# Taking the reciprocal roots of the 128-column norms on GpSimd instead of ScalarE and VectorE

## The chip, the cores and the metric

The kernel runs on one core of a Trainium2 chip. A core has TensorE (matrix multiply, PE in the profile), VectorE (DVE), ScalarE (ACT), GpSimd (POOL) and SyncE (SP, which here only starts transfers). Each engine works through its own instruction list in order, and they wait for each other through semaphores. The metric is the device time of one execution in microseconds.

## The reference

Two transformer layers over x of shape (8, 256, 128), that is 2048 rows of 128 columns, all in float32. Each layer has an attention block and a feed-forward block, and after each block the sum with its input is normalized:

```python
def _layernorm(x, axis=-1, eps=1e-05):
    m = jnp.mean(x, axis=axis, keepdims=True)
    v = jnp.var(x, axis=axis, keepdims=True)
    return (x - m) / jnp.sqrt(v + eps)

x = _layernorm(x + _L0_attn_ref(x, ...), axis=-1)   # Taylor-exp linear attention, 16 heads, RMS norm per head
x = _layernorm(x + _L0_ffn_ref(x, ...), axis=-1)    # top-1 of 2 experts plus a shared one, relu
x = _layernorm(x + _L1_attn_ref(x, ...), axis=-1)   # softmax attention, 16 heads of 8, rotary, causal
x = _layernorm(x + _L1_ffn_ref(x, ...), axis=-1)    # top-2 of 8 experts, silu gate
```

## The kernel before

The 2048 rows are worked in four groups (g = 0 to 3) of 512 rows; a group is a tile of 128 partitions by four row blocks of 128 columns. Layer 0's attention runs over eight batches with four steps each. As its groups become ready, layer 0's feed-forward network (`ffn0`, names ph, hq, pf), layer 1's attention (sa, sb, pr, pa, mx, qm) and layer 1's routed network (pg, sg, hT, pd, yg) follow, interleaved.

The routed network of a group works so: `gates`, `ranks` and `places` compute each row's two slots; GpSimd writes the rows to their slots in DRAM by indirect transfers (`sent`, L1025, slots<-x_b, for the last group slots<-pay); SP loads the slots in chunks (xg<-slots) and the weights of each slot tile's expert (we<-in_e, L1293); TensorE computes pg (L1329), ScalarE the silu (sg, L1335), VectorE the product hT (L1336), TensorE pd (L1353), and ScalarE copies yg out, which SP stores to DRAM (answers<-yg). For groups 0 to 2 GpSimd then gathers each row's two answers (L1417, yb<-answers); VectorE sums them, norms them, and SP stores the result (out<-yb). For the last group GpSimd scatters the answers (L1381), SP loads them, and two halves of the group are summed and normed.

A norm is made by `spreads` and `scaled_rows`. `spreads` takes mean and variance of each of the four row blocks on VectorE (L283, L284, into mv), the root of variance plus epsilon on ScalarE (L286, into sd) and its reciprocal on VectorE (L288, into rs). `scaled_rows` then subtracts and multiplies on VectorE, four instructions (L297). There are seventeen such norms: four of layer 0's attention (tiles named a), four of its network (f), four of layer 1's attention (b) and five of its network (o: groups 0, 1 and 2, and two halves of group 3, which have two row blocks each). The RMS norms inside layer 0's attention (L473, L481) are others, with 32 columns, and keep their root on ScalarE.

[...]The compiler puts an ACT_TABLE_LOAD ahead of an activation whose function isn't in the set at hand. In layer 1 ScalarE also computes Exp (L907, L1149), Tanh (L1339) and Silu (L1335), so that the root has loads on both sides there; a load is shown under the line of the activation that it stands before.

The order of the work: in layer 0's attention the lists of TensorE, ScalarE, VectorE and SP are in the order in which the program is written; in the second half TensorE's alone is, by the slot table of `second_half`, and a scheduler orders the other engines. GpSimd's list is the scheduler's throughout.

Of the kernel before, what the change touches and what calls it, by code (L numbers as in the profile page):

```python
# [11 lines left out]
F32 = mybir.dt.float32  # L12
BF16 = mybir.dt.bfloat16
I32 = mybir.dt.int32
AF = mybir.ActivationFunctionType
ALU = mybir.AluOpType
AX = mybir.AxisListType

P = 128
B, T, D = 8, 256, 128  # L20
NT = B * T // P
TG = 4
# [13 lines left out]
LN_EPS = 1e-5  # L36
# [43 lines left out]
def network(  # L80
# [19 lines left out]
    nc = tc.nc  # L100
# [3 lines left out]
    cpool = ctx.enter_context(tc.tile_pool(name="const", bufs=1))  # L104
# [3 lines left out]
    spool = ctx.enter_context(tc.tile_pool(name="stat", bufs=4))  # L108
# [122 lines left out]
    def column(name, value):  # L231
        t = cpool.tile([P, 1], F32, tag=name, name=name)
        nc.gpsimd.memset(t, value)
        return t

    eps_ln = column("eps_ln", LN_EPS)
    eps_rms = column("eps_rms", RMS_EPS)
    rt_half = column("rt_half", math.sqrt(0.5))


# [34 lines left out]
    def layernorm(r, name, y=None):  # L275
        return scaled_rows(r, name, spreads(r, name), y)

    def spreads(r, name):
        n = r.shape[1]
        mv = spool.tile([P, n, 2], F32, tag="mv", name=f"mv_{name}")  # L280
        for t in range(n):
            st = spool.tile([P, 6], F32, tag="bn", name=f"bn_{name}_{t}")
            nc.vector.bn_stats(st, r[:, t, :])  # L283
            nc.vector.bn_aggr(mv[:, t, :], st)  # L284
        sd = spool.tile([P, n], F32, tag="sd", name=f"sd_{name}")
        nc.scalar.activation(sd, mv[:, :, 1], AF.Sqrt, bias=eps_ln)  # L286
        rs = spool.tile([P, n], F32, tag="rs", name=f"rs_{name}")
        nc.vector.reciprocal(rs, sd)  # L288
        return mv, rs

    def scaled_rows(r, name, spread, y=None):
# [309 lines left out]
    def ffn0(g, buf, pbank, obank, even):  # L601
# [50 lines left out]
        def ended():  # L652
            pt = pbank(f"pb_{g}")
            for t in range(TG):
                w = slice(t * P, (t + 1) * P)
                nc.tensor.transpose(pt[:, w], got["y"][:, w], ident)
            r = got["r"] = gpool.tile([P, TG, D], F32, tag="r", name=f"r1_{g}")
            nc.vector.tensor_add(r, pt.rearrange("p (t d) -> p t d", t=TG), xs[g])
            got["s"] = spreads(r, f"f{g}")
# [47 lines left out]
    def second_half():  # L707
# [262 lines left out]
        def ended1(b):  # L970
            g, s = b // 2, b % 2
            yT = yTs.pop(b)
            po = bank(f"pz_{b}")
            for q in range(2):
                nc.tensor.matmul(
                    po[:, q * P : (q + 1) * P],
                    yT[:, q * P : (q + 1) * P],
                    wo1_sb,
                    start=True,
                    stop=True,  # L980
                )
            if s == 0:
                rs[g] = gpool.tile([P, TG, D], F32, tag="r", name=f"r2_{g}")
            nc.vector.tensor_add(
                rs[g][:, 2 * s : 2 * s + 2, :],
                po[:, : 2 * P].rearrange("p (q d) -> p q d", q=2),
                xs[g][:, 2 * s : 2 * s + 2, :],
            )
            if s == 1:
                at(6 * (b + 2) + 4, normed1, g, spreads(rs[g], f"b{g}"))  # L990
# [603 lines left out]
```

## Time and profile before

| | us |
|---|---|
| median of 3 runs | 611.17 (610.21 to 614.69) |
| the profiled execution | 610.17 |
| its span, first to last instruction | 608.4 |
| ScalarE: ACT_TABLE_LOAD | 21 of 1.283 each |
| ScalarE: root of a norm (sd) | 17 of 0.297 each |
| VectorE: reciprocal of a norm (rs) | 17 of about 0.18 each |
| GpSimd: indirect transfers L1025, L1417, L1381 | 71, 0.96 to 0.99 each |

The granted TensorE clock was 0.938 on average. In the profile a row of the timeline gives the start, the duration, the engine, the line, the operation with its tiles, how many were merged, and in brackets how long the engine was idle before and what ended that. The chain of waits is the work that ended last, followed backwards from the end; "issue" in it is time in which nothing that the profile shows was waited for. The slices cut the span in 40 equal parts of 15.2 us.

### The profile page before, as it was taken

The page shows a single profiled execution, that of the slowest core. Times are in us where ns is not written, and L with a number is a line of the kernel's source. Part 1 is how long each engine was busy: PE and PEld are TensorE (multiplying, and loading weights), DVE is VectorE, ACT ScalarE, POOL GpSimd, SP SyncE. Part 2 cuts the span into 40 slices and gives each one's busy share as a digit, 9 for nine tenths or more (in the row PEclk, how much of TensorE's full clock was granted, in tenths as well). Part 3 has the DMA queues.
Part 4 walks back from the last instruction along what each step waited for, and adds up shares of the span by engine and source line. Part 5 has one row for each costly group of instructions (what it writes and reads, how often), then busy time and mean ns, then how long its engine had stood idle before and what let it go on. Part 6 is the DMA issues. An engine that isn't in the chain of part 4 may idle for free.

```text
span 608.4 us, 10761 instructions
## 1 busy us (share of the span) xinstructions
PE 524.0 (86%) x4194; PEld 340.6 (56%) x4194; DVE 327.6 (54%) x759; ACT 248.1 (41%) x367; POOL 170.1 (28%) x208
## 2 busy tenths in 40 slices
PE   5799999999989999899989989899999859748750
PEld 2455656666654544344554546456678659748740
DVE  2346678478565162744564555746955436632424
ACT  2276444636341124144446344345547318322130
POOL 5022212222230030012213112452172540451670
PEclk9799999999999999989999996799999879998785
DMA  9106803230250000000000000231226357729512
GB/s 321 61 1 170 216 19 70 71 72 6 66 141 0 1 0 2 0 2 0 1 1 1 1 1 2 75 100 32 70 94 195 105 154 211 233 82 260 168 41 70
DMA packets 40562, 47.34 MB, mean 78 GB/s; under 512 B 3655, under 2 KB 29404, under 8 KB 39488
## 3 DMA queue, kind: packets, MB, share of 16 engines
q1 hardware_dynamic: 37520, 40.33, 23.8%
q0 software_dynamic: 2560, 5.02, 2.5%
q10 hardware_dynamic: 432, 1.31, 0.6%
q8 instruction: 34, 0.56, 0.4%
q14 instruction: 16, 0.13, 0.1%
HBM read 35.95 MB, written 11.15 MB: 77 GB/s over the span
## 4 chain that ended last, share of the span: by engine, by line
PE 65%; DVE 14%; POOL 6%; DMA 5%; ACT 5%; issue 4%; SPq 1%; POOLq 0%; ACTq 0%; DVEq 0%
PE pf L640 6%; PE pg L1329 6%; PE ph L622 5%; PE pv L356 5%; PE py L436 5%; PE sb L897 4%; PE pd L1353 4%; PE po L516 4%; DVE mx L860 4%; PE sa L828 3%; PE s L397 3%; PE pr L758 3%; POOL yb L1417 2%; PE pa L930 2%; PE py L444 2%
## 5 line engine op out<-in xcount | busy, mean ns | idle before, releaser
L1329 PE MATMUL pg<-xTs,we 128*128 128x128 f32 x480 | 66.8, 293 | 26.7 <-DVE hT L1336 14.5
L1329 PEld LDWEIGHTS pg<-xTs,we 128*128 128x128 f32 x480 | 61.7, 206 | 29.5 <-DVE hT L1336 15.5
L909 POOL TENSOR_SCALAR_AFFINE_SELECT pr<-pr 128x512 f32<-128x512 f32 (+1 forms) x48 | 37.7, 795 | 127.7 <-ACT pr L907 127.4
L460 POOL TENSOR_TENSOR y<-y 128x512 f32<-128x512 f32 x32 | 35.1, 1096 | 135.3 <-DVE y L453 103.4
L860 DVE TENSOR_REDUCE mx<-sa 128x4 f32<-128x1024 f32 (+1 forms) x48 | 56.5, 1219 | 27.3 <-PE sa L851 19.7
L414 DVE SCALAR_TENSOR_TENSOR at<-at,causal 128x1024 f32<-128x1024 f32 x32 | 39.2, 1225 | 42.2 <-ACT at L413 42.0
L413 ACT ACTIVATE at<-s,rt_half 128x1536 f32<-128x1536 f32 x32 | 49.2, 1536 | 17.7 <-PE s L405 17.7
L907 ACT ACTIVATE pr<-sb 128x1024 f32<-128x1024 f32 x48 | 46.5, 1021 | 17.3 <-PE sb L897 17.2
L897 PE MATMUL sb<-qm,kr 32*128 32x128 f32 (+1 forms) x512 | 34.6, 353 | 8.1 <-DVE mx L860 7.9
L436 PE MATMUL py<-at,v 128*64 128x256 f32 x256 | 41.1, 400 | 0.6 <-DVE at L414 0.3
L356 PE MATMUL pv<-wv,xt 128*128 128x512 f32 x64 | 35.3, 652 | 2.1 <-DVE kT L349 1.4
L640 PE MATMUL pf<-hq,w 128*128 128x512 f32 x72 | 37.0, 605 | 0.0
L516 PEld LDWEIGHTS po<-wo_sb,y 128*128 128x128 f32 x256 | 30.8, 192 | 9.6 <-issue 4.2
L1353 PE MATMUL pd<-e,hT 128*128 x240 | 35.1, 292 | 0.6 <-issue 0.3
L897 PEld LDWEIGHTS sb<-qm,kr 32*128 32x128 f32 x512 | 22.8, 189 | 20.1 <-DVE mx L860 17.2
L1417 POOL DMA_INDIRECT yb<-answers,slot_i x24 | 23.0, 960 | 39.4 <-DMA answers<-yg 27.2
L516 PE MATMUL po<-wo_sb,y 128*128 128x128 f32 x256 | 32.1, 278 | 1.9 <-DVE st L471 1.5
L1353 PEld LDWEIGHTS pd<-e,hT 128*128 128x128 f32 x240 | 31.5, 203 | 1.9 <-issue 1.1
L1025 POOL DMA_INDIRECT slots<-x_b,slot_i x24 | 23.3, 971 | 27.9 <-DVE nets L1244 22.2
L1335 ACT ACTIVATE sg<-pg 128x512 f32<-128x512 f32 (+1 forms) x24 | 13.5, 563 | 36.6 <-PE pg L1329 36.5
L930 PE MATMUL pa<-pr,vaug 128*32 128x128 f32 (+1 forms) x512 | 28.3, 338 | 0.0
L634 DVE TENSOR_SCALAR hq<-ph,sml 128x512 f32<-128x512 f32 x20 | 14.9, 749 | 22.7 <-PE ph L622 22.7
(228 smaller groups left out, 932.6 us busy)
## 6 DMA issues: line engine op xcount, KB each, us to landing
we<-in_e SPq DMA_DIRECT2D x60, 256.0 KB, 3.3
bc<-nr SPq DMA_DIRECT2D x14, 512.0 KB, 5.6
slots<-empty SPq DMA_DIRECT2D x3, 960.0 KB, 10.3
answers<-yg SPq DMA_DIRECT2D x21, 128.0 KB, 3.1
xg<-slots SPq DMA_DIRECT2D x9, 256.0 KB, 3.4
w<-in_w SPq DMA_DIRECT2D x2, 768.0 KB, 7.1
xt<-in_xt SPq DMA_DIRECT2D x4, 256.0 KB, 9.3
x<-in_x SPq DMA_DIRECT2D x4, 256.0 KB, 8.8
```

The source lines that it names most:

```text
L356: nc.tensor.matmul(pv, xT[:, t * P : (t + 1) * P], wv_sb[:, w], start=True, stop=True)
L413: nc.scalar.activation(at, ps[:, :, 0:SC], AF.Square, bias=rt_half, scale=SQ_SCALE)
L414: nc.vector.scalar_tensor_tensor(at[:, :, 0 : 2 * P], at[:, :, 0 : 2 * P], 0.5, causal.unsqueeze(1).broadcast_to([P, 4, 2 * P]), ALU.add, ...
L436: nc.tensor.matmul(py[o, cc], v[:, 0, w], at[:, i, :].rearrange("p (a q) -> p a q", q=P)[:, 0::2, :], start=True, stop=False,)
L516: nc.tensor.matmul(po, ys[b, c // 2][:, c % 2, q * P : (q + 1) * P], wo_sb[:, c, :], start=(c == 0), stop=(c == 7),)
L640: nc.tensor.matmul(got["o"], w2_sb[:, k * P : (k + 1) * P], hq.pop(n), start=(n == 0), stop=(n == 11),)
L860: nc.vector.tensor_reduce(mx[:, 2 * h : 2 * h + 2, 3 * js.start : 3 * js.stop - 2 : 3], ps[h].rearrange("p i (j k) -> p i j k", j=js.stop ...
L897: nc.tensor.matmul(ps[i // 2][:, i % 2, jj * wd : (jj + 1) * wd], kT[r, j, k], qms[b][r, j // 3, q], start=True, stop=True,)
L907: nc.scalar.activation(w, ps[h], AF.Exp)
L930: nc.tensor.matmul(pa[r, jj, :] if m == 0 else pa[r, jj, P:T], va[:, t + m, 4 * i + j, :], prs[b, jp][:, i, jj * T : (jj + 1) * T] if m == ...
L1329: nc.tensor.matmul(ph[:, b, cw], w[:, cw], x, start=True, stop=True)
L1353: nc.tensor.matmul(po[:, a * P : (a + 1) * P], hT[m][:, a, c * P : (c + 1) * P], e3_sb[:, bass.ds(net_i, 1), c * D : (c + 1) * D].rearrang ...
```

## The change

The column of LN_EPS is gone, and a tile of four columns of -0.5 is filled once. In `spreads` GpSimd adds the epsilon to the variance and raises the sum to the power of -0.5; the root on ScalarE, the reciprocal on VectorE and the tile sd are gone.

```diff
-    eps_ln = column("eps_ln", LN_EPS)
     eps_rms = column("eps_rms", RMS_EPS)
+    minus_half = cpool.tile([P, TG], F32, tag="minus_half", name="minus_half")
+    nc.gpsimd.memset(minus_half, -0.5)
     rt_half = column("rt_half", math.sqrt(0.5))
...
             nc.vector.bn_stats(st, r[:, t, :])
             nc.vector.bn_aggr(mv[:, t, :], st)
-        sd = spool.tile([P, n], F32, tag="sd", name=f"sd_{name}")
-        nc.scalar.activation(sd, mv[:, :, 1], AF.Sqrt, bias=eps_ln)
         rs = spool.tile([P, n], F32, tag="rs", name=f"rs_{name}")
-        nc.vector.reciprocal(rs, sd)
+        nc.gpsimd.tensor_scalar_add(rs, mv[:, :, 1], LN_EPS)
+        nc.gpsimd.tensor_tensor(rs, rs, minus_half[:, :n], ALU.pow)
         return mv, rs
```

In the built order of the changed kernel GpSimd has 34 instructions more, ScalarE 32 fewer (17 roots and 15 table loads) and VectorE 17 fewer. TensorE's order is unchanged. On SP the store out<-yb of group 1 and one answers<-yg store move ahead of the first xg load of group 3, and two weight loads with them. On GpSimd the two new instructions of a norm stand where the scheduler put them among the old ones; those of group 1's last norm stand behind the eight scatters slots<-pay.

## The prediction

> **What bounds the kernel now.** I read four views: the page's busy table with its slices, the chain that ended last, each engine's timeline around the seventeen norms, and the built order of both kernels.
>
> ```profile
> PE 524.0 (86%) x4194; PEld 340.6 (56%) x4194; DVE 327.6 (54%) x759; ACT 248.1 (41%) x367; POOL 170.1 (28%) x208
> PE   5799999999989999899989989899999859748750
> PEclk9799999999999999989999996799999879998785
> POOL 5022212222230030012213112452172540451670
> ```
>
> TensorE is full to about 480 us (slice 32), then has holes. Up to there a norm costs only what it delays on a chain of VectorE work that feeds TensorE. After it the chain is a queue on GpSimd:
>
> ```profile
> 521.73 1.28 ACT L1335 ACT_TABLE_LOAD   x1 [3.39 <-PE pg L1329]
> 528.21 1.28 ACT L286 ACT_TABLE_LOAD   x1
> 535.48 0.30 ACT L286 ACTIVATE sd_o<-mv_o,eps_ln 128x4 f32<-128x4 f32 x1 [5.99 <-DVE mv_o L284]
> 535.80 1.28 ACT L1335 ACT_TABLE_LOAD   x1
> ...
> 522.78 0.95 POOL L1417 DMA_INDIRECT yb<-answers,slot_i  x1 [27.21 <-DMA answers<-yg]
> ...
> 532.79 0.99 POOL L1025 DMA_INDIRECT slots<-pay,slot_i  x1 [0.30 <-issue]
> ...
> 541.69 0.96 POOL L1025 DMA_INDIRECT slots<-pay,slot_i  x1 [0.30 <-issue]
> 547.01 0.19 POOL L1312 COPY gs<-xg 128x4 f32<-128x4 f32 x1 [4.36 <-DMA xg<-slots]
> 547.14 0.18 POOL L1314 CAST di<-xg 128x4 int32<-128x4 f32 x1
> ```
>
> Two things: ScalarE sits from 528.2 to 535.5 at a root whose input is late, with its queue shut behind it; and GpSimd issues sixteen transfers in a row, 1.26 us apart, up to 542.65. The chain shows what one norm costs, first a plain one, then one behind a table load:
>
> ```profile
> 176.16 0.30 ACT sd_a L286
> 176.47 0.02 issue
> 176.49 0.19 DVE rs_a L288
> 176.68 0.03 issue
> 176.71 1.11 DVE x_a L297 x4
> ...
> 359.53 1.28 ACT L286
> 360.81 0.01 issue
> 360.83 0.30 ACT sd_b L286
> ```
>
> **The change part by part.** Removed: 17 roots on ScalarE of 0.30 us, 17 reciprocals on VectorE of 0.18, and, by the built order, 15 of the 21 table loads, 15 x 1.28 = 19.2 us of ScalarE. Added: 17 additions and 17 powers on GpSimd. The totals matter little, since neither engine is the bound; the latency from the statistics to the scaling of the rows does.
>
> Old latency: 176.14 (statistics end) to 176.71, 0.57 us. New latency: GpSimd wakes 0.07 us after VectorE (chain, 226.98 to 227.05 before rk), the addition takes 0.19 (the 128x4 COPY above), a hand-over of about 0.1 (taken from that wake-up) since the built order has the power wait on GpSimd's own semaphore, the power w, and 0.04 to wake VectorE: 0.40 + w.
>
> No row shows a power. From below it is the COPY of the same shape, 0.19. From above I use the row[...]: an indirect transfer makes its 128 descriptors in about 0.96 us, 7.5 ns each, so 512 powers taken one by one would be 3.8 us, 4.0 with the fixed part. The elementwise row L460 costs 1096 ns for 512 columns, 2.1 ns a column. If a power is a chain of some forty such steps (an assumption), four columns cost 0.34, so w = 0.19 + 0.34, about 0.5. I take 0.5, as the work is elementwise like L460, and keep 0.19 and 4.0. Then the new latency is 0.90, 0.33 more than the old.
>
> Norms, in time order, for w = 0.5:
> - Layer 0 attention, 96.4 and 137.2: the scaled rows aren't needed at once, but the causal multiply L414 stands behind them on VectorE and starts at 98.22 with no idle before it; TensorE's L436 follows it at once. The root is also taken off ScalarE, where L413 waited behind it, but VectorE's own order hides that. 0.2 each, 0.4. The third (176.1) is on the chain: 0.33.
> - First routed-network norm (215.3): in the new order its addition and power on GpSimd stand on either side of the second vaug memset (1.8 us), and its scaling on VectorE comes after x0T and one hq; the transpose that needs it runs at 221.16. The cover of some 4 us is nearly used up: 0.5. The attention norm at 220.5 is covered by 2.82 us of VectorE idle before 225.31; without that it would cost 0.33.
> - The next three of these (253.9, 305.4, 366.6) are on the chain: 3 x 0.33 = 1.0. The loads around 303 and 310 save no chain time that the trace shows.
> - Layer 1 norm at 358.9: GpSimd is in affine_select until 359.64, then 0.19 + 0.1 + 0.5 + 0.04 gives scaling at 360.47 instead of 361.37: 0.9 saved. At 415.3 likewise: affine_select until 415.80, scaling at 416.63 instead of 416.95: 0.3 saved. At 459.5 TensorE leads the chain on both sides: 0.
> - 503.6 to 512.8: four loads and two roots (5.7 us) leave ScalarE, which was busy 8.82 of 9.20 us; but TensorE was busy 9.02 of it, so what shows is its small gap at 512.5 to 512.8 and a little after: 0.5 saved. Both powers run before GpSimd's gathers resume at 522.78, with 10 us to spare.
> - 522.8 to 542.65: sixteen issues on GpSimd, untouched: 0.
> - Group 1's last norm (535.45): its addition is built behind the eight scatters, so VectorE, in order, stands until about 543.6 where it went on at 536.0. Behind it wait hT (537.72 before), so the next pg on TensorE, and on SP the out store. The order of SP changes too: that store, an answers store and two weight loads now come ahead of xg, which stood first. The weight load that ended TensorE's wait at 548.48 was issued at 544.97; it now goes at about 546.6 and lands after 3.47, at 550.1: 1.6 late. Against that, pg of the units before it now runs at 544.6 to 548.4, directly ahead, so TensorE is warm for what comes next, which took 2.08, 1.71 and 1.60 us in the cold stretch at 548.48 (granted clock 0.84 over 545 to 566) and about 0.9 each elsewhere: up to 2.7 back. I book 0, between -0.5 and +2.
> - Tail after 598.02: three norms one after another. VectorE now stands at each (in the new order the first scaling is ahead of the second half's statistics): 3 x 0.33, plus some 0.3 for statistics that no longer fill the gaps: 1.3.
>
> Sum: 0.4 + 0.33 + 0.5 + 1.0 - 0.9 - 0.3 - 0.5 + 0 + 1.3 = +1.8 us. The profiled execution took 610.17 (span 608.4), so 612.0; the median of 611.17 is 1.0 above it, so 613. Some twelve norms lie where w counts one for one (two, one, three, two, one and three above), so each us of w is worth 12 us: w = 0.19 gives 609, w = 0.86 makes +6, w = 2 gives 631, w = 4 gives 655.
>
> **Two rules of the Trainium skill.** The rows: the load at 415.11 begins 0.02 after the exp before it and the root starts at 416.40, 1.29 later, no drain in between. "ScalarE: Activation LUTs", What ACT_TABLE_LOAD costs, adds a drain of 1.38 us to every switch, 2.66 in all. By that, each of the two layer 1 norms would gain 1.38 more and the sum would be -1.0; by the trace it is +1.8. I use the trace. The rule that speaks against the change: the first y of L460 on GpSimd (28.22) took 1.04 us, like the later ones. "GPSIMD Engine Reference", Instruction dispatch, says that the first call of a freshly loaded routine pays about 6 us, unseen in a profile. If the power were such a routine, VectorE would stand some 6 us at the first norm, and the sum would be +7.8, 619. No loading row of GpSimd is in this trace, so I book nothing for it.
>
> **Rivals.** (1) The power is slow. Place: the VectorE queue at twelve norms. Price: 12 us for each us of w above 0.5. It decides from w = 0.86, where the loss passes 1%. Likely case w = 1.5, 625. For: no row shows a power cheap, and the page's GpSimd rows cost 1.6 times VectorE's for the same tile (L460 1096 ns, L507 686 ns where not held up). Against: only four columns. (2) ScalarE's freed time counts in full: 0.9 + 1.3 at the layer 1 norms, 5.7 at 503 to 513 and half of the 7.3 us stall at 528 to 535: about 9 less, 602. For: ScalarE is in the chain at 510.16 with a load. Against: TensorE was 98% busy there, and VectorE's new stall replaces ScalarE's old one. (3) The place behind the scatters is not made up for by a warm TensorE: 2 us there, and the later xg load and the answers stores behind it 4 more: 619. That the change doesn't do what it says is ruled out by the built order.
>
> **How the numbers follow.** About 1% (6.1 us) is what can be told from no change here. Chances: forecast 0.46, slow power 0.37, queue place 0.08, ScalarE in full 0.09. So faster 0.09, same 0.46, slower 0.45. The forecast's own range is 608 to 617; the range goes from 605, short of rival 2, to 630, w near 2, which leaves out about 2 in 10.
>
> **What would show it.** A row for the power on GpSimd with its mean (0.5, or over 0.86); VectorE idle before the scaling, ended by GpSimd, of 0.6 to 0.8 at plain norms; six table loads left; that idle of some 8 us once, near 535 to 543, with the out store ahead of xg on SP; pg after 550 at 0.9 instead of 2.08. I am wrong if a plain norm costs no more than 0.57, or if the stretch from 522 to 556 shrinks or grows by more than 2 us.

## The result, and the profile after

The changed kernel takes 627.99 us (median of six runs, 625.85 to 628.42) against 611.56 for the kernel before in the same session: a ratio of 1.0258, interval 1.0229 to 1.0288. The profiled execution took 625.85, its span is 623.9, 15.5 more than before. The sum of the prediction, +1.8 us, was made for a power of 0.5 us. The loss came as its first rival describes it, and is about twice what that rival's price gives for the power that was measured.

The page of the changed kernel, its lines for the engines' busy time and for the chain of waits:

```profile
PE 524.7 (84%) x4194; PEld 340.3 (55%) x4194; DVE 324.7 (52%) x742; ACT 225.4 (36%) x335; POOL 192.4 (31%) x242
PE 62%; DVE 16%; POOL 8%; DMA 5%; issue 4%; ACT 3%; SPq 1%; POOLq 0%; ACTq 0%; DVEq 0%
```

ScalarE lost 22.7 us of work and GpSimd gained 22.3; TensorE works as long as before (524.0). No engine has become the bound. GpSimd is busy for 31% of the span, and whoever had read only this line would call that harmless. What has changed is who waits. This is the answer for the power's line of the changed kernel, count, minimum, median and maximum in ns, and below it the idle time in us that instructions spent waiting for it, with their number:

```profile
L288 POOL TENSOR_TENSOR rs_o<-rs_o,minus_half x5: 709/1032/1042, 517.8 to 615.7; 128x4 f32<-128x4 f32 x3, 128x2 f32<-128x2 f32 x2
L288 POOL TENSOR_TENSOR rs_a<-rs_a,minus_half x4: 1033/1040/1047, 96.2 to 226.0; 128x4 f32<-128x4 f32 x4
...
  DVE yb L297: 12.1, 5
  DVE x_a L297: 5.9, 4
  DVE x_b L297: 5.3, 3
  DVE x_f L297: 4.4, 3
  DVE pay L297: 1.1, 1
```

(The dots stand for the lines of the f and b norms.) A power of four columns takes 1.03 to 1.05 us, one of two columns 0.71. The first, at 96.2, took as long as the others and VectorE waited 1.49 us for it, so the first-call price of 6 us that the prediction weighed is not seen here. VectorE stood idle for 28.8 us in front of the scaling. In the kernel before it waited for the root, and the same answer for ScalarE's root (L286) has, in front of VectorE's reciprocals:

```profile
  DVE rs_b L288: 4.7, 4
  DVE rs_o L288: 2.4, 3
  DVE rs_f L288: 1.7, 4
  DVE rs_a L288: 1.1, 3
```

That is 9.9 us. One plain norm shows it in full. From the timeline of GpSimd and of VectorE in the changed kernel (start, duration; in brackets the idle time before and what ended it):

```profile
95.86 0.23 POOL L287 TENSOR_SCALAR rs_a<-mv_a 128x4 f32<-128x4 f32 x1 [2.14 <-DVE mv_a L285]
96.17 1.05 POOL L288 TENSOR_TENSOR rs_a<-rs_a,minus_half 128x4 f32<-128x4 f32 x1
...
97.25 1.11 DVE L297 TENSOR_SCALAR x_a<-r,mv_a,rs_a 128x128 f32<-128x128 f32 x4 [1.49 <-POOL rs_a L288]
```

From the last statistics (95.76) to the scaling are 1.49 us, where the kernel before needed 0.57. ScalarE and VectorE made root and reciprocal in 0.30 + 0.19; GpSimd takes 0.23 + 1.05, and 0.31 lie between the starts of its two instructions.

### The profile page after: what moved, and what is told of

It reads as the page before. It is cut to its first block, busy times and chain, and to the rows that moved or that the text cites. A ratio compares the mean times of both kernels' runs of the same rounds, so it can differ in the third digit from the quotient of the medians.

```text
span 623.9 us, 10734 instructions
## 1 busy us (share of the span) xinstructions
PE 524.7 (84%) x4194; PEld 340.3 (55%) x4194; DVE 324.7 (52%) x742; ACT 225.4 (36%) x335; POOL 192.4 (31%) x242
## 4 chain that ended last, share of the span: by engine, by line
PE 62%; DVE 16%; POOL 8%; DMA 5%; issue 4%; ACT 3%; SPq 1%; POOLq 0%; ACTq 0%; DVEq 0%
PE pf L640 6%; PE pg L1329 6%; PE ph L622 5%; PE pv L356 5%; PE sb L897 4%; PE py L436 4%; DVE mx L860 4%; PE po L516 4%; PE pd L1353 4%; PE sa L828 3%; PE pr L758 3%; PE s L397 2%; PE pa L930 2%; POOL yb L1417 2%; POOL slots L1025 2%
## 5 line engine op out<-in xcount | busy, mean ns | idle before, releaser
L1329 PE MATMUL pg<-xTs,we 128*128 128x128 f32 x480 | 65.5, 291 | 30.9 <-DVE hT L1336 24.8
L860 DVE TENSOR_REDUCE mx<-sa 128x4 f32<-128x1024 f32 (+1 forms) x48 | 56.5, 1220 | 27.7 <-PE sa L851 19.9
L897 PE MATMUL sb<-qm,kr 32*128 32x128 f32 (+1 forms) x512 | 36.9, 369 | 9.6 <-DVE mx L860 9.4
L897 PEld LDWEIGHTS sb<-qm,kr 32*128 32x128 f32 x512 | 24.6, 202 | 21.8 <-DVE mx L860 18.9
```

The lines of the kernel that those rows point to most:

```text
L860: nc.vector.tensor_reduce(mx[:, 2 * h : 2 * h + 2, 3 * js.start : 3 * js.stop - 2 : 3], ps[h].rearrange("p i (j k) -> p i j k", j=js.stop ...
L897: nc.tensor.matmul(ps[i // 2][:, i % 2, jj * wd : (jj + 1) * wd], kT[r, j, k], qms[b][r, j // 3, q], start=True, stop=True,)
L1329: nc.tensor.matmul(ph[:, b, cw], w[:, cw], x, start=True, stop=True)
```

## The experiments

Three theories had to be told apart. A: the power's own length, waited for by VectorE at some twelve norms, is the loss. B: the loss is a fixed cost of using GpSimd (its place in the queue, its end), whatever the operation takes. C, a part of B: the program waits at its end for GpSimd. Theory D, at o1_old below, is the place in the queue alone. For the other half of the change there is the question whether the time that ScalarE gained is worth anything. Each run was timed beside the kernel before on the same chip; "us" below is a ratio times 610.5.

| kernel | median us | ratio to before | interval |
|---|---|---|---|
| changed kernel | 627.99 | 1.0258 | 1.0229 to 1.0288 |
| two_powers | 647.55 | 1.0615 | 1.0589 to 1.0641 |
| cheap_pool | 615.28 | 1.0080 | 1.0053 to 1.0107 |
| no_root | 607.58 | 0.9950 | 0.9927 to 0.9973 |
| late_pool | 613.51 | 1.0051 | 1.0032 to 1.0071 |
| layer0_old | 618.03 | 1.0118 | 1.0078 to 1.0158 |
| o1_old | 625.93 | 1.0267 | 1.0227 to 1.0306 |
| tail_old | 622.58 | 1.0192 | 1.0153 to 1.0232 |
| layer1_pow | 611.58 | 1.0017 | 0.9994 to 1.0041 |
| a_old | 625.34 | 1.0269 | 1.0241 to 1.0296 |
| split_all | 643.08 | 1.0571 | 1.0532 to 1.0611 |
| split_b | 631.10 | 1.0349 | 1.0325 to 1.0373 |
| split_late | 636.05 | 1.0440 | 1.0418 to 1.0462 |

### Longer and shorter: two_powers and cheap_pool

```diff
-    nc.gpsimd.memset(minus_half, -0.5)
+    nc.gpsimd.memset(minus_half, 0.5)
+    minus_one = cpool.tile([P, TG], F32, tag="minus_one", name="minus_one")
+    nc.gpsimd.memset(minus_one, -1.0)
...
         nc.gpsimd.tensor_tensor(rs, rs, minus_half[:, :n], ALU.pow)
+        nc.gpsimd.tensor_tensor(rs, rs, minus_one[:, :n], ALU.pow)
```

> Two powers of GpSimd in place of one at every 128-column norm (root by +0.5, then reciprocal by -1), one behind the other, the same values out. It lengthens every norm by one more power, 1.05 us for 4 columns as in the profile of after, and changes nothing else. Theory A (the time of the power, waited for by VectorE at some 12 norms, carries the loss): 12 x 1.05 = 12.6 us over the changed kernel, about 640.5 us, 1.047 of the kernel before. Theory B (the loss is fixed: the place in GpSimd's queue, a colder TensorE clock, the late end of GpSimd): the norms absorb most of it, at most 5 us over the changed kernel, under 633 us.

```diff
-    nc.gpsimd.memset(minus_half, -0.5)
+    nc.gpsimd.memset(minus_half, 0.7)
...
-        nc.gpsimd.tensor_scalar_add(rs, mv[:, :, 1], LN_EPS)
-        nc.gpsimd.tensor_tensor(rs, rs, minus_half[:, :n], ALU.pow)
+        nc.gpsimd.tensor_scalar_mul(rs, mv[:, :, 1], 1e-6)
+        nc.gpsimd.tensor_tensor(rs, rs, minus_half[:, :n], ALU.add)
```

> The changed kernel with its power replaced by an addition of the same tile on GpSimd, and the sum before it by a multiplication: the factor of a norm is 0.7 + 0.000001 x variance in place of one over the root of the variance. Order, engines, waits and places in the queues stay as in the changed kernel. The short GpSimd rows are 0.23 to 0.36 us, so the operation should take about 0.3 us and not 1.05. Theory A: 0.75 us less x 12 = 9 us off, about 619 us, 1.012 of the kernel before. The prediction's own sum at 0.3 us would give 610.6. Theory B (fixed costs of the place and of the end): at most 4 us off, 624 us or more.

The second power took 1.01 us, the addition of cheap_pool 0.20. The same answer as above, for the line of the power's place in cheap_pool:

```profile
L288 POOL TENSOR_TENSOR rs_a<-rs_a,minus_half x4: 198/198/199, 98.7 to 225.0; 128x4 f32<-128x4 f32 x4
...
  DVE yb L297: 8.9, 4
  DVE x_b L297: 3.1, 3
  DVE x_a L297: 2.5, 4
  DVE x_f L297: 1.9, 3
  DVE pay L297: 0.2, 1
```

and for the second power of two_powers:

```profile
L291 POOL TENSOR_TENSOR rs_a<-rs_a,minus_one x4: 1006/1006/1012, 100.3 to 234.9; 128x4 f32<-128x4 f32 x4
...
  DVE yb L300: 16.8, 5
  DVE x_a L300: 10.2, 4
  DVE x_f L300: 8.7, 4
  DVE x_b L300: 8.6, 3
  DVE pay L300: 2.1, 1
```

In cheap_pool the traces show the same order on TensorE, VectorE, ScalarE and SP as in the changed kernel; its norms have other values, so that rows may go to other experts, but it has the same number of matmuls and moves as many bytes (47.3 MB). In two_powers one load xg and one store out<-yb change places on SP besides. VectorE's wait is 16.6, 28.8 and 46.4 us, the time above the kernel before 4.9, 15.8 and 37.5 us. From cheap_pool to the changed kernel the operation is 0.84 us longer and the kernel 10.9 longer: 13 us for each us, with an interval of about 3. That is theory A's price, and B, which gave at most 4 us, falls as the main cause. It keeps at most the 4.9 us of cheap_pool, of which some 3 have a cause that late_pool shows below; the other 2 are about as large as the intervals. From the changed kernel to two_powers it is 21.8 us for about 1.08 us of latency, near 20 for each us, more than A's 12: waits alone grew by 17.6, and TensorE's own busy time by 9.3 (534.0 against 524.7). The granted clock was 0.913 to 0.916 in all four runs of two_powers and 0.923 to 0.931 in the six of the changed kernel. So TensorE worked more slowly where it stood more often; that the standing is the reason is not shown by these means alone. One place comes below.

### What ScalarE's gain is worth: no_root

```diff
-        nc.scalar.activation(sd, mv[:, :, 1], AF.Sqrt, bias=eps_ln)
+        nc.scalar.activation(sd, mv[:, :, 1], AF.Identity, bias=eps_ln)
```

> The kernel before with ScalarE's root of the 128-column norms replaced by a plain scaled copy with the same bias (the norms then divide by the variance, not by its root): the instruction, its waits and VectorE's reciprocal stay, and what goes is the switch of ScalarE's function for the root. The prediction's view, that what ScalarE gains is hidden: within 2 us of the kernel before, 610 to 612 us. Its second rival, that ScalarE's freed time counts in full: about 602 us, 0.985.

Six table loads are left of 21, and ScalarE's busy time falls from 248.1 to 228.7 us. The kernel gains 3.1 us (1.6 to 4.5). So 19 us of loads are not hidden entirely, nor do they count in full; both expectations missed, the first by little. The 3.1 us are not the loads alone: the scheduler also placed some of VectorE's scalings and reciprocals and two stores of SP elsewhere than in the kernel before. As it stands, it is the best measure here of what a norm without loads could bring.

### GpSimd's end: late_pool

```diff
         def spread(ts):
             got["s", ts.start] = spreads(got["y"][:, ts, 0, :], f"o{g}{ts.start}")
+            if g == NG - 2:
+                late = spool.tile([P, TG], F32, tag="late", name="late", bufs=1)
+                nc.gpsimd.tensor_copy(late, got["s", ts.start][1])
```

> The kernel before with one short GpSimd copy (128x4) of the factor of the next-to-last output norm, so that GpSimd's last operation comes some 10 us later than its last scatter; nobody reads it. Theory C (the program ends only some 6.4 us after GpSimd's last operation, which in the kernel before is hidden behind the output stores): the span grows by about 2 us, 613.5 us, 1.003. Rival: GpSimd's end costs nothing and the time stays, 611.5 us, 1.000.

One copy of 0.2 us that nobody reads costs 3.1 us (2.0 to 4.3). The trace holds a DRAIN of GpSimd at the end of the program. The line of the program's end, first in the kernel before, then in the changed kernel, then in late_pool (minimum, median, maximum in ns; the maximum is the drain that follows GpSimd's last work, and the first time is its start):

```profile
L1590 POOLq DRAIN  x3: 46/104/13279, 587.4 to 608.1; - x3
```

```profile
L1590 POOLq DRAIN  x3: 46/104/7457, 615.6 to 623.6; - x3
```

```profile
L1593 POOLq DRAIN  x3: 46/104/6587, 603.4 to 610.5; - x3
```

Start and length give its end: 600.64, 623.07, 609.95. GpSimd's last operation ended at 594.28, 616.69 and 603.57, so the drain ends 6.4 us behind it each time. In the kernel before SP was done with the output at 607.59, long after the drain. In the changed kernel SP was done at 620.61 and the program waited for the drain, 2.5 us; in late_pool 607.25 and 2.7. Theory C stands.

### By parts: layer0_old, tail_old, o1_old, layer1_pow, a_old

Each of these chooses by the norm's name which of the two ways it takes; the edit is one condition in `spreads`, and the column of LN_EPS again. Here is that of layer0_old:

```diff
+    eps_ln = column("eps_ln", LN_EPS)
...
-        nc.gpsimd.tensor_scalar_add(rs, mv[:, :, 1], LN_EPS)
-        nc.gpsimd.tensor_tensor(rs, rs, minus_half[:, :n], ALU.pow)
+        if name[0] in "bo":
+            nc.gpsimd.tensor_scalar_add(rs, mv[:, :, 1], LN_EPS)
+            nc.gpsimd.tensor_tensor(rs, rs, minus_half[:, :n], ALU.pow)
+        else:
+            sd = spool.tile([P, n], F32, tag="sd", name=f"sd_{name}")
+            nc.scalar.activation(sd, mv[:, :, 1], AF.Sqrt, bias=eps_ln)
+            nc.vector.reciprocal(rs, sd)
```

> The changed kernel with the norms a0 to a3 and f0 to f3 (the first eight) back on ScalarE's root and VectorE's reciprocal; the b and o norms stay on GpSimd's power. In the traces TensorE stands 7.1 to 7.5 us later than in the kernel before when the f norms are through. Theory A (every power that VectorE waits for is paid where it stands, and the pieces add): 7.5 us less than the changed kernel, about 619 us, 1.013 of the kernel before. Rival (the delay would be taken up later by waits for GpSimd and for DMA, so the norms of layer 1 and the end carry the loss): 2 us less at most, 625 us, 1.022.

> The changed kernel with the norms o2 and o3 (three norms at the end, 128x2, 128x2 and 128x4) back on ScalarE and VectorE, so that GpSimd's last operation is again a scatter. Theory A + C (the waits for the power, 0.6 + 0.6 + 0.9, and the end of GpSimd, 2.5): 4.6 us less than the changed kernel, about 622.5 us, 1.018. Theory A alone, without a cost of GpSimd's end: 2.1 us less, 625 us, 1.022.

> The kernel before with GpSimd's power only at the norms b0 to b3 and o0, where ScalarE's root in the kernel before needs a switch of its function (a load of 1.28 us ahead of it); all other norms as before. By the waits: VectorE waits some 1.2 us for the root at a b norm in the kernel before and 1.3 to 1.5 for the power in the changed one, and ScalarE's loads for the root and back go: between 1 us less and 2 us more than the kernel before, 610 to 613 us, 0.998 to 1.003. If the place on GpSimd were what costs, 3 us or more above it, 1.005 or more.

layer0_old is 8.5 us faster than the changed kernel, tail_old 4.0; layer1_pow is 1.0 us above the kernel before (0.4 below to 2.5 above). Their sum is 13.5 of the 15.8 us, with some 3 us of uncertainty on each of the first two: as far as that goes, the parts add. The 4.0 of tail_old do not by themselves decide between the two sizes that were expected, 4.6 and 2.1, but its trace tells the end apart from the waits: from the end of its last scaling (618.73) to the end of the program are 3.6 us, in the changed kernel 6.0 (617.84 to 623.9), in the kernel before 3.6. So 2.4 of the gain is the drain.

> The changed kernel with only the norms a0 to a3 back on ScalarE and VectorE. layer0_old, which moves the f norms too, took 8.5 us off. By the traces TensorE is 2.9 us late after the a norms (0.5 for a0, 0.7 for a1, 2.2 for a2, less 0.5 of start): about 3 us less than the changed kernel, 624.5 us, 1.021, so that the f norms carry 5 to 6. Rival: the clock that TensorE gets is what is lost at f2, and the a norms are taken up by it: under 1.5 us.

a_old missed what was expected of it: 1.021 lies outside its interval, and its ratio is not below that of the changed kernel, though its profiled span is 2.4 us shorter. Taken together the intervals allow from 2 us less to 3 more, and why the 3 us did not come stays open. How layer 0's 8.5 us divide between the a and the f norms is therefore read from the traces alone. Compared matmul by matmul, in the order that all these kernels share, TensorE falls behind the kernel before by 3.6 us at the a norms, by 0.8 at f1 and by 3.9 at f2. A part of that is the clock, and differs from trace to trace.

At f2 the trace of the changed kernel loses most. TensorE's timeline around it, in the kernel before:

```profile
308.01 0.49 PE L897 MATMUL sb<-qm,kr 32*128 32x128 f32 x4 [0.77 <-DVE mx L860]
309.14 1.16 PE L897 MATMUL sb<-qm,kr 32*128 32x128 f32 x28 [0.64 <-DVE mx L860]
310.23 1.09 PE L948 MATMUL pyt<-ident,ya 128*128 128x128 f32 x8
311.65 1.10 PE L622 MATMUL ph<-xT_f,w 128*128 128x512 f32 x2 [0.33 <-DVE y L956]
```

and in the changed kernel, with VectorE's scaling ahead of it:

```profile
310.48 1.12 DVE L297 TENSOR_SCALAR x_f<-r,mv_f,rs_f 128x128 f32<-128x128 f32 x4 [1.48 <-POOL rs_f L288]
...
312.79 0.49 PE L897 MATMUL sb<-qm,kr 32*128 32x128 f32 x4 [1.94 <-DVE mx L860]
313.92 2.08 PE L897 MATMUL sb<-qm,kr 32*128 32x128 f32 x28 [0.64 <-DVE mx L860]
315.93 1.97 PE L948 MATMUL pyt<-ident,ya 128*128 128x128 f32 x8
317.81 2.05 PE L622 MATMUL ph<-xT_f,w 128*128 128x512 f32 x2
```

The attention's maximum (mx, L860) stands behind the scaling on VectorE, and TensorE stands behind the maximum: it waits 1.94 instead of 0.77, 1.2 us more. Then the same three groups of matmuls take 2.08, 1.97 and 2.05 instead of 1.16, 1.09 and 1.10, 2.75 us more. The windows of the changed kernel (length, then busy time of PE, PEld, DVE, ACT, POOL, then the granted clock) say why. They are cut at the moments at which the clock changed in this trace, in steps of 3.41 us:

```profile
310.27:313.68 3.41, 1.07 (x20) 0.53 (x12) 3.20 (x6) 1.11 (x2) 0.18 (x1) 1.00 0.00 0
313.68:317.09 3.41, 3.17 (x34) 2.95 (x35) 0.20 (x2) 1.38 (x2) 0.28 (x1) 0.50 0.00 0
317.09:320.50 3.41, 3.41 (x7) 1.58 (x6) 1.62 (x5) 0.56 (x1) 1.86 (x2) 0.50 0.00 0
320.50:323.91 3.41, 3.41 (x26) 1.76 (x25) 1.83 (x5) 0.00 (x0) 0.00 (x0) 1.00 0.00 0
```

Behind a stretch of 3.41 us in which TensorE was busy for 1.07, the clock was halved for 6.8 us. But the 2.75 us are not the price of the power. In late_pool f2 is normed as in the kernel before, with the same gap of 0.77 us in front of the maximum's matmuls, and the clock was halved there too, for one such stretch:

```profile
305.28:308.69 3.41, 1.99 (x26) 0.85 (x28) 3.37 (x7) 1.27 (x2) 0.00 (x0) 1.00 0.00 0
308.69:312.10 3.41, 3.41 (x36) 3.14 (x36) 0.50 (x3) 1.84 (x2) 0.00 (x0) 0.50 0.00 0
```

Its three groups take 1.99, 1.86 and 1.10, 4.95 in all, 1.6 us more than in the kernel before. The five other traces with the old f2 divide likewise: 4.94 to 4.96 us in layer1_pow, no_root, layer0_old and split_b, and 3.35 only in the kernel before. Of the four traces with one power at f2, o1_old, tail_old and a_old have 4.91 to 4.95, and only the changed kernel 6.10. What does come with the power is the wait, 1.93 or 1.94 us against 0.77 to 1.03 with the old f2. So of the 3.9 us at f2, 1.2 are shown to be the power's; the rest is clock, which differs between traces with one and the same f2.

The gap's length alone doesn't decide over the clock: with 1.08 us in cheap_pool and 1.72 in split_late it stayed at 1.00. The Trainium skill ("TensorE: Matmul & The Clock Gate", Part 1) has the clock set by a free-running window of some 3.4 us, which fits the steps of 3.41 us. But it speaks of an idle window, and in late_pool one with 1.99 us of work in it was followed by the halved clock, while in split_late one with 1.69 (303.09 to 306.50) was not. What decides is not shown.

At a2 (2.2 us of the 3.6) the wait is 0.9: TensorE stands 1.09 us in front of pf in the changed kernel and 0.19 in the kernel before. The other 1.3 lie ahead of the norm, in a stretch of halved clock from 170.3 to 173.7. Such a stretch is there in late_pool and layer0_old as well, which then have none some 25 us later, where the kernel before and the changed kernel have one. The changed kernel, o1_old, tail_old and two_powers have two such stretches between 165 and 210, the ten other traces one; why is not shown.

> The changed kernel with only the norm o1 (the output norm that stands behind sixteen scatters in GpSimd's queue) back on ScalarE and VectorE. The prediction's booking (its delay of TensorE, 8 us at 540 us in the trace, is recovered by 553 us): within 1.5 us of the changed kernel, 626 to 628 us. Theory D (the place behind the scatters carries what the power's length does not explain): 4 to 6 us less, about 622 us, 1.018.

o1_old changes nothing that the intervals of some 3 us would show: 1.0267 against 1.0258. The stall that it takes away is the longest of all. In the changed kernel, GpSimd, VectorE and TensorE around it:

```profile
550.96 0.97 POOL L1025 DMA_INDIRECT slots<-pay,slot_i  x1 [0.30 <-issue]
551.96 0.25 POOL L287 TENSOR_SCALAR rs_o<-mv_o 128x4 f32<-128x4 f32 x1
552.30 1.04 POOL L288 TENSOR_TENSOR rs_o<-rs_o,minus_half 128x4 f32<-128x4 f32 x1
...
553.38 0.60 DVE L297 TENSOR_SCALAR yb<-yb,mv_o,rs_o 128x128 f32<-128x128 f32 x2 [8.81 <-POOL rs_o L288]
...
554.63 3.78 PE L1329 MATMUL pg<-xTs,we 128*128 128x128 f32 x16 [10.69 <-DVE hT L1336]
...
559.69 1.95 PE L1329 MATMUL pg<-xTs,we 128*128 128x128 f32 x16
```

TensorE in o1_old:

```profile
549.86 2.05 PE L1335 MATMUL pg<-xTs,we 128*128 128x128 f32 x16 [2.51 <-DVE hT L1342]
...
560.26 2.08 PE L1335 MATMUL pg<-xTs,we 128*128 128x128 f32 x8 [6.56 <-DMA we<-in_e]
```

VectorE's 8.81 us and TensorE's 10.69 are real, and TensorE goes on 4.8 us sooner in o1_old. But then it stands 6.56 us for the next expert's weights and starts on them at 560.26, where the changed kernel starts at 559.69. The stall lies beside that transfer. What the changed kernel loses in starting later it gets back in clock: its sixteen matmuls at 559.69 take 1.95 us, the eight of o1_old at 560.26 take 2.08. TensorE in o1_old ran 2.6 us behind the changed kernel at 525 us (since its first matmuls, ahead of any norm), 4.8 ahead at 550, and 2.4 behind again at 566. So 8.8 of VectorE's 28.8 us cost nothing that shows. cheap_pool has the same wait at this place, 7.6 of its 16.6.

### Less wait, more work: the halves

```diff
+        for h in range(0, n, 2):
+            m = min(2, n - h)
+            mv = spool.tile([P, m, 2], F32, tag=f"mv{h}", name=f"mv{h}_{name}")
...
+            rs = spool.tile([P, m], F32, tag=f"rs{h}", name=f"rs{h}_{name}")
+            nc.gpsimd.tensor_scalar_add(rs, mv[:, :, 1], LN_EPS)
+            nc.gpsimd.tensor_tensor(rs, rs, minus_half[:, :m], ALU.pow)
```

> The changed kernel with each 128-column norm's sum and power in two halves of two columns, the first given to GpSimd as soon as the first two spreads stand, while VectorE makes the other two. GpSimd works longer (0.71 us for a power of 128x2, twice, in place of 1.03 for one of 128x4), VectorE waits less: the first half is ready about when the last spread is, the second some 1.3 us after it, of which two scalings cover 0.6. Theory A (what counts is VectorE's wait, not GpSimd's work): 0.8 us less wait at some 12 norms, at 13 us per us, about 10 us less than the changed kernel, 617 us, 1.010. Rival (GpSimd's work, its places in the queue): not less than the changed kernel, 627 us or more, 1.026.

> As layer1_pow (power only at b0 to b3 and o0), but in the two halves. Theory A: 0.8 us less wait at five norms than layer1_pow, 3 to 4 us less, 0.995 to 0.997 of the kernel before: faster than both kernels. Rival: the five norms are covered by other waits of layer 1, no less than layer1_pow, 1.001 to 1.002.

> The two halves of a power at f2, f3, b0 to b3, o0 and o1, the other norms on ScalarE's root: all loads of ScalarE for the root but the last are gone. Theory A: as split_b or up to 1 us less, 0.993 to 0.997. Rival: f2, f3 or o1 lose on GpSimd what the loads bring, 1.000 or more.

All three are slower than expected; split_b is some 20 us slower than the same norms in one piece (layer1_pow). The design worked where it was made for: VectorE's wait at the four a norms is 3.2 us in split_all, 5.9 in the changed kernel. It failed at the b norms, whose two powers stand 22 to 26 us apart, and where the order of VectorE is the scheduler's. It put the scaling of the first half right behind its statistics. GpSimd and VectorE in split_b:

```profile
396.20 0.96 POOL L1045 DMA_INDIRECT slots<-x_b,slot_i  x1 [0.30 <-issue]
397.19 0.25 POOL L306 TENSOR_SCALAR rs_b<-mv_b 128x2 f32<-128x2 f32 x1
397.62 1.02 POOL L1045 DMA_INDIRECT slots<-x_b,slot_i  x1 [0.18 <-issue]
398.66 0.74 POOL L307 TENSOR_TENSOR rs_b<-rs_b,minus_half 128x2 f32<-128x2 f32 x1
...
399.44 0.60 DVE L317 TENSOR_SCALAR x_b<-r,mv_b,rs_b 128x128 f32<-128x128 f32 x2 [9.24 <-POOL rs_b L307]
```

The statistics were ready at 390.2, but the addition stands behind the scatters that run until 397, the power behind one more, and VectorE waits 9.24 us in front of a scaling that layer1_pow does only with the second half. Behind it waits the attention's maximum, and TensorE for that, 9.04 us. Three such waits (9.24, 8.72, 7.80) make 25.8 of the 33.9 us that split_b spends waiting for its powers. Theory A as such is not touched, since VectorE's wait did not shrink. But the rival, the place in GpSimd's queue, which cost nothing at o1, is the dear one here, where TensorE stood for the maximum alone. No version beats the kernel before; layer1_pow only equals it.

## Why the prediction was right, and where not

The time lies within the range of the prediction and on the side of its second largest chance. Its own case fell, and its first rival came. That the number lies inside the range is in part luck: at the power that was measured, the prediction's own arithmetic gives 613 + 6.4 = 619, and terms that it did not have make up the rest to 628. The rival's example (w = 1.5, 625) is close by chance too, with a longer power and without those terms. By its steps:

- **The power, w = 0.5.** This is the term that failed, at "a chain of some forty such steps (an assumption)". The rows give 1.04 us for four columns and 0.71 for two, so about 0.38 fixed and 0.165 a column; the sum had 0.19 and 0.085. Both parts were half of what they are. The bound of 3.8 us was not reached either; it was drawn from an indirect transfer, of whose inner work no trace shows anything.
- **The latency, 0.40 + w.** Held: 1.49 measured at a plain norm for w = 1.05, 0.65 in cheap_pool for 0.20.
- **The cost of a wait.** Held where it can be seen alone: TensorE's delay at a0, a1, a2 and f1, without the clock at a2, is 0.7, 0.7, 0.9 and 0.8 us, where the sum at w = 1.03 has 0.7, 0.7, 0.9 and 0.9. At f2 it is 1.2 for 0.9.
- **Twelve us for each us of w.** Held up to the changed kernel (13, give or take 3), too low beyond it (near 20). With w = 1.03 the sum is +1.8 + 0.53 x 12 = +8.2, the rival's own figure; the runs give 15.8, give or take 1.8.
- **What it lacked.** GpSimd's drain, which no step had: 2.5 us by the trace, 3.1 in late_pool. The last operation on GpSimd was moved from 594 to the very end, and the sum asked only what waits for the power, not what waits for GpSimd's end. With it, and with the 1.0 us of layer1_pow in place of the gains of the next step, the sum comes to about 12.5. The other 3 us are hardly more than the uncertainty of these terms taken together; the clock at a2 and f2 may be in them, but no run measures it alone. Of the 15.5 us between the two profiled spans, 1.3 at a2 and 2.75 at f2 are clock, and single executions begin unlike as well: at 90 us, ahead of all norms, TensorE is between 0.9 us ahead and 2.3 behind the kernel before in the traces of this case.
- **Gains at the layer 1 norms, -0.9, -0.3 and -0.5.** Not confirmed. layer1_pow, which has just these, is 1.0 us above the kernel before, where the sum at w = 1.03 comes to between -0.6 and 0; the interval holds both.
- **The tail, 1.3 at w = 0.5, 2.9 at 1.03.** Held: the time from the last scatter's start to the end of the last scaling grew from 11.5 to 14.1 us, by 2.6.
- **o1 behind the scatters, 0.** Held within the 3 us that o1_old's interval leaves, and for the two reasons that were given: the wait for the weights that stands there anyway, and a TensorE at full clock after it. That came later than was thought: the sixteen matmuls of pg at 554.63 took 3.78 us, the next sixteen 1.95. The stretch from 522 to 556, in the kernel before from the px at 521.61 to that at 555.94, takes 34.3 us there and 35.5 in the changed kernel (530.28 to 565.77); the growth is less than the 2 us that would have spoken against the prediction. Rival 3 falls with it.
- **ScalarE's freed time.** no_root measures 3.1 us for the loads, a third of rival 2's 9. (The gains listed for that rival add to some 11.5, and the costs of the sum to 3.5, so its net is 8.) It is within the changed kernel's account already and was paid several times over.

## What to carry to other kernels

An engine that is 28% busy is no place to move work to for that reason: for a short operation between two instructions of one engine, compare latencies, hand-over included, and multiply by the number of places where the waiting engine leads the chain. Of an unmeasured operation the per-column cost and the fixed cost both need a row; where neither is there, time that one operation first. And before work is put last on an engine, ask what the end of the program waits for on it, and what already stands in its queue when the work becomes ready.

## What the runs showed of the hardware

GpSimd's drain at the end of the program ended 6.4 us after its last operation in three kernels, whether that was a scatter, a power or a copy of 0.2 us. A power of GpSimd costs 1.04 us for 128x4 and 0.71 for 128x2, an addition of 128x4 0.20. At one and the same place (f2) TensorE's clock was halved for 3.4 or 6.8 us in eleven of the fourteen traces, with the old norm and with the new, and stayed at full speed in three. So one trace of each kernel is not enough to put such a loss down to a change.
